# Block transposes on VectorE and DMAs between quadrants in place of TensorE transposes, in a two-layer graph kernel

## The chip, the cores and the metric

The kernel runs on one core of a Trainium2 chip. The metric is device time in microseconds (us); the time of a kernel is the median of its runs.

## The reference

x is 128 batches of 128 tokens by 512 features, adj is one 128 by 128 matrix, all float32. Both layers add a residual and normalize each row (mean and variance over the 512 features, eps 1e-5).

```
# layer 0
A = adj @ x[b];  C = adj @ x[b] + bias[:, None]
pre[o, m, n] = A[o, n] + (C - A)[o, m]
x1 = layernorm(x + max_n relu(pre))
# layer 1: 8 heads of 64, mask = adj
q, k, v = split(x1 @ w_qkv)
attn = softmax(where(adj == 0, -inf, q k^T / 8))
o = (attn @ v) @ w_proj + b_proj
out = layernorm(x1 + o + (layernorm(o) * gamma + beta))
```

In layer 0, both products use the same matrix, so C - A is the bias of the row and the maximum over n is the row maximum of adj @ x.

## The kernel before

All 128 batches pass through one software pipeline on the five engines. A tile holds one batch: 128 partitions (tokens) by 512 features. Batches go in groups of G = 4, whose 512 tokens form one moving operand for the projections to Q and K. The whole program is unrolled: the loop over steps s runs over the batches, and in one step TensorE works on different batches at different stages, as listed at the bottom of the kernel. A compiler layer derives the waits between engines and may reorder instructions of one engine by its own estimate of when they are ready.

In a step of the body TensorE runs, in this order: `scores` of batch s (pss, L198); one Q/K unit of the next group (pq, L158: four products of 128 by 128 by 512, each recorded as two instructions); `prob_transpose` of batch s - 1 (ptp, eight 128 by 128 transposes against the identity, L243); `layer0` of batch s + 9 (pa, L121); the second Q/K unit; `attend` of s - 1 (po, L255); `layer0_transpose` of batch s + 8 (ptx, four transposes, L147); `v_unit` (pv, L174); `project` of s - 1 (pp, L272). A matrix product contracts over the partitions, so the probabilities p and the layer-0 output x1 must be transposed before they can be operands: `prob_transpose` makes pT, read by `attend`, and `layer0_transpose` makes x1T, read by `qk_unit` and `v_unit`. Both write PSUM tiles, which ScalarE (L148, L245) and VectorE (L247) copy to SBUF.

Softmax: VectorE scales and masks the scores (L207) and takes the row maxima (L216), ScalarE runs eight exponentials (L222) with their sums, VectorE divides (L233, L235). Layer 0 after its product: a row maximum on VectorE (amax, L123), l0t = pa + bias on ScalarE (L125), minus pa on VectorE (L126), relu with amax on ScalarE (l0r, L128), plus x on GpSimd (y, L130). `stats` and `normalize` (L101 to L113) serve all layernorms, with the power on GpSimd; the tail of layer 1 uses GpSimd for gamma, beta and the sum (L285 to L287).

Transfers: x comes in by groups of four batches (1 MB each, L75) and the output leaves by batches (256 KB, L298), both on the queue of SP, in order; the weights are issued at the start on ScalarE's queue.

Of the kernel before, what the change touches and what calls it, by code (L numbers as in the profile page):

```python
# [16 lines left out]
def kernel(  # L17
# [12 lines left out]
    """Two residual+layernorm graph layers, software-pipelined over the batch.  # L30

    Batches go in groups of G, whose tokens share the moving operand of the
    Q/K projections. In step s the tensor engine works on
      batch s:             attention scores
      batch s - 1:         attention * V and the output projection
      group of s, plus 1:  a share of the Q/K/V projections
      batch s + 2G:        transposition of its layer-0 output
      batch s + 2G + 1:    the layer-0 product with adj
    so that each of these finds its operands ready.
    """  # L40
    nc = tc.nc
# [6 lines left out]
    NP = H // 2  # L48
    EPS = 1e-5
# [5 lines left out]
    ps_s = ctx.enter_context(tc.tile_pool(name="ps_s", bufs=2, space=bass.MemoryType.PSUM))  # L55
    ps_t = ctx.enter_context(tc.tile_pool(name="ps_t", bufs=2, space=bass.MemoryType.PSUM))
    ps_m = ctx.enter_context(tc.tile_pool(name="ps_m", bufs=3, space=bass.MemoryType.PSUM))
    ps_o = ctx.enter_context(tc.tile_pool(name="ps_o", bufs=1, space=bass.MemoryType.PSUM))

# [11 lines left out]
    xg = {}  # L71

    def load(g):
        t = sb.tile([P, G, D], F32, tag="xg", name=f"xg_{g}")
        nc.sync.dma_start(out=t, in_=x[ts(g, G)].rearrange("b p d -> p b d"))  # L75
        xg[g] = t

    load(0)
    load(1)

# [11 lines left out]
    # adj^T, and the additive mask: 0 on edges, and where adj is 0 a number so low  # L92
    # that exp(score - row maximum) is 0
    adjT = const.tile([P, P], F32, name="adjT")
    pt0 = ps_t.tile([P, KC, P], F32, tag="pt", name="pt0")
# [4 lines left out]

    def stats(src, name):  # L101
        """mean and (var + eps)^-0.5 of each row: [P, 2]"""
        st = small.tile([P, 6], F32, tag="st", name=f"st_{name}")
        nc.vector.bn_stats(st, src)  # L104
        mv = small.tile([P, 2], F32, tag="mv", name=f"mv_{name}", bufs=8)
        nc.vector.bn_aggr(mv, st)  # L106
        rs = small.tile([P, 1], F32, tag="rs", name=f"rs_{name}", bufs=8)
        nc.gpsimd.tensor_scalar(rs, mv[:, 1:2], EPS, None, ALU.add)  # L108
        nc.gpsimd.tensor_tensor(rs, rs, mhalf, ALU.pow)  # L109
        return mv, rs  # L110
# [5 lines left out]
    ys, y_st, x1s, x1T = {}, {}, {}, {}  # L116

    def layer0(f):
        xin = xg[f // G][:, f % G, :]
        pa = ps_m.tile([P, D], F32, tag="pm", name=f"pa_{f}")  # L120
        nc.tensor.matmul(pa, lhsT=adjT, rhs=xin, start=True, stop=True)  # L121
        amax = small.tile([P, 1], F32, tag="amax", name=f"amax_{f}")
        nc.vector.tensor_reduce(amax, pa, AX.X, ALU.max)  # L123
        t = sb.tile([P, D], F32, tag="l0t", name=f"l0t_{f}")
        nc.scalar.activation(t, pa, AF.Identity, bias=bias0)  # L125
        nc.vector.tensor_tensor(t, t, pa, ALU.subtract)  # L126
        r = sb.tile([P, D], F32, tag="l0r", name=f"l0r_{f}")
        nc.scalar.activation(r, t, AF.Relu, bias=amax)  # L128
        y = sb.tile([P, D], F32, tag="y", name=f"y_{f}")
        nc.gpsimd.tensor_tensor(y, xin, r, ALU.add)  # L130
        ys[f] = y
# [4 lines left out]
    def layer0_norm(f):  # L136
        x1 = sb.tile([P, D], F32, tag="x1", name=f"x1_{f}", bufs=2 * G + 6)
        normalize(x1, ys.pop(f), *y_st.pop(f))
        x1s[f] = x1

    def layer0_transpose(f):
        g, j = divmod(f, G)
        if j == 0:
            x1T[g] = sb.tile([P, KC, GT], F32, tag="x1T", name=f"x1T_{g}")
        pt = ps_t.tile([P, KC, P], F32, tag="pt", name=f"ptx_{f}")
        for c in range(KC):
            nc.tensor.transpose(pt[:, c, :], x1s[f][:, ts(c, P)], ident)  # L147
        nc.scalar.copy(x1T[g][:, :, ts(j, P)], pt)  # L148

# [1 line left out]
    qkT, vs = {}, {}  # L151

    def qk_unit(g, m):
        if m == 0:
            qkT[g] = sb.tile([P, 2 * KC, GT], F32, tag="qkT", name=f"qkT_{g}")
        pq = ps_m.tile([P, GT], F32, tag="pm", name=f"pq_{g}_{m}")
        for c in range(KC):
            nc.tensor.matmul(  # L158
                pq,
                lhsT=wqkv[:, c, ts(m, P)],  # L160
                rhs=x1T[g][:, c, :],
                start=(c == 0),
                stop=(c == KC - 1),
            )
        if m % 2 == 0:
            nc.scalar.copy(qkT[g][:, m, :], pq)
        else:
            nc.vector.tensor_copy(qkT[g][:, m, :], pq)

    def v_unit(f):  # L170
        g, j = divmod(f, G)
        pv = ps_m.tile([P, D], F32, tag="pm", name=f"pv_{f}")
        for c in range(KC):
            nc.tensor.matmul(  # L174
                pv,
                lhsT=x1T[g][:, c, ts(j, P)],
                rhs=wqkv[:, c, ds(2 * D, D)],
                start=(c == 0),
                stop=(c == KC - 1),
            )  # L180
        v = sb.tile([P, D], F32, tag="v", name=f"v_{f}", bufs=G + 3)
        nc.scalar.copy(v, pv)
        vs[f] = v

# [1 line left out]
    # Even and odd heads sit on the two halves of the array's rows and so write  # L186
    # to different PSUM banks: [:, parity, pair] is head 2 * pair + parity.
    sc, prob, psum_, pT, oT = {}, {}, {}, {}, {}

    def scores(b):  # L190
# [4 lines left out]
        for pr in range(NP):  # L195
            for par in range(2):
                rows = ds(par * HD, HD)
                nc.tensor.matmul(  # L198
                    pss[par][:, pr, :],
                    lhsT=qkT[g][rows, pr, ts(j, P)],  # L200
                    rhs=qkT[g][rows, KC + pr, ts(j, P)],
                    start=True,
                    stop=True,
                )
        s = sb.tile([P, 2, NP, P], F32, tag="s", name=f"s_{b}")
        for par in range(2):
# [9 lines left out]
        nc.vector.tensor_reduce(  # L216
            nmax, s.rearrange("p a h m -> p (a h) m"), AX.X, ALU.max, negate=True
        )
        sums = small.tile([P, H], F32, tag="sums", name=f"sums_{b}")
        p = sb.tile([P, 2, NP, P], F32, tag="prob", name=f"p_{b}")  # L220
        for i in range(H):
            nc.scalar.activation(  # L222
                p[:, i // NP, i % NP, :],
                s[:, i // NP, i % NP, :],
                AF.Exp,
                bias=nmax[:, i : i + 1],
                accum_out=sums[:, i : i + 1],
            )
        prob[b], psum_[b] = p, sums

    def softmax_div(b):
        rec = small.tile([P, H], F32, tag="rec", name=f"rec_{b}")
        nc.vector.reciprocal(rec, psum_.pop(b))  # L233
        p = prob[b].rearrange("p a h m -> p (a h) m")
        nc.vector.tensor_tensor(p, p, rec.unsqueeze(2).to_broadcast([P, H, P]), ALU.mult)  # L235

    def prob_transpose(b):
        p = prob.pop(b)
        t = sb.tile([P, 2, NP, P], F32, tag="pT", name=f"pT_{b}")
        for par in range(2):  # L240
            pt = ps_t.tile([P, NP, P], F32, tag="pt", name=f"ptp_{b}_{par}")
            for pr in range(NP):
                nc.tensor.transpose(pt[:, pr, :], p[:, par, pr, :], ident)  # L243
            if par == 0:
                nc.scalar.copy(t[:, par], pt)  # L245
            else:
                nc.vector.tensor_copy(t[:, par], pt)  # L247
        pT[b] = t

    def attend(b):  # L250
        v, t = vs.pop(b), pT.pop(b)
        po = ps_o.tile([P, NP, P], F32, tag="po", name=f"po_{b}")
        for pr in range(NP):
            for par in range(2):
                nc.tensor.matmul(  # L255
                    po[ds(par * HD, HD), pr, :],
                    lhsT=v[:, ds((2 * pr + par) * HD, HD)],
                    rhs=t[:, par, pr, :],
                    start=True,
                    stop=True,  # L260
                )
# [6 lines left out]
    def project(b):  # L268
        o = oT.pop(b)
        pp = ps_m.tile([P, D], F32, tag="pm", name=f"pp_{b}")  # L270
        for c in range(KC):
            nc.tensor.matmul(  # L272
                pp, lhsT=o[:, c, :], rhs=wproj[:, c, :], start=(c == 0), stop=(c == KC - 1)
            )
# [29 lines left out]
    for s in range(-(2 * G + 1), B + 4):  # L304
        g, j = divmod(s, G)
        nxt = g + 1
        has_next = 0 <= nxt < B // G
        on(scores, s)
        on(tail_outer, s - 3)
        on(layer0_norm, s + 2 * G)  # L310
        if has_next:
            qk_unit(nxt, 2 * j)
        on(prob_transpose, s - 1)
        on(layer0, s + 2 * G + 1)
# [4 lines left out]
        on(layer0_transpose, s + 2 * G)  # L319
        if has_next:  # L320
            v_unit(s + G)
        on(layer0_stats, s + 2 * G + 1)
        on(project, s - 1)
        on(softmax_div, s)
        on(tail_residual, s - 2)
        f = s + 2 * G + 1
        if f % G == G - 1 and 2 <= f // G + 2 < B // G:
            load(f // G + 2)
# [41 lines left out]
```

## Time and profile before

| | |
|---|---|
| median of 3 runs | 2444.42 us (2443.89 to 2444.57) |
| profiled execution, span | 2444.3 us |
| profiled execution around the span | nothing that shows: span and median agree within 0.2 us |
| TensorE busy | 2381.0 us, 97% of the span |
| VectorE / ScalarE / GpSimd busy | 59% / 37% / 39% |
| transfers | 73.95 MB, mean 30 GB/s; SP's queue takes 8.0% of the 16 DMA engines |
| granted TensorE clock, mean | 0.990 |

Times in the profile are of one execution. "Busy" sums the instructions of an engine; "idle before" is the time in which an engine waited ahead of a group of instructions, with what released it. The chain of work that ended last follows the execution back from its last instruction, at each step to what released it.

### The profile page before, as it was taken

Reading aid. Unit: us, or ns where it says so; the run is one execution under the profiler, and the core shown is the slowest. Engines: PE = TensorE matmul, PEld = TensorE weight load, DVE = VectorE, ACT = ScalarE, POOL = GpSimd, SP = SyncE. Lnnn points to the kernel's source line nnn. Section 1 sums busy time; section 2 is a strip of 40 time slices with the busy share of each in tenths; the row PEclk is TensorE's granted clock in tenths of the full one; section 3 lists DMA queues with packets and bytes.
Section 4 is the critical chain, followed back from the end, with each engine's and each line's share of the span. In section 5 each row is a group of like instructions: output and inputs, shape, how many; then the busy total and the mean of one; then the engine's idle time right before and its main releaser. Section 6 shows DMA issues by size and latency. Waiting matters only on the chain.

```text
span 2444.3 us, 28218 instructions
## 1 busy us (share of the span) xinstructions
PE 2381.0 (97%) x9985; PEld 1205.6 (49%) x9985; DVE 1449.8 (59%) x2562; ACT 899.4 (37%) x2945; POOL 951.7 (39%) x1287
## 2 busy tenths in 40 slices
PE   5999999999999999999999999999999999999995
PEld 2455455555555555545555555555554554555443
DVE  3465565666666656556566666666655656656556
ACT  2334334334333333333433433333333343343232
POOL 2134334334334334433433433433443343343335
PEclk8999999999999999999999999999999999999997
DMA  3000000000000001000000100100100000000000
GB/s 134 18 31 31 31 32 17 31 31 35 31 31 18 31 31 35 30 25 22 33 31 31 35 14 31 35 31 31 35 14 31 34 32 31 31 18 14 14 18 26
DMA packets 37292, 73.95 MB, mean 30 GB/s; under 512 B 2848, under 2 KB 2976, under 8 KB 37152
## 3 DMA queue, kind: packets, MB, share of 16 engines
q1 hardware_dynamic: 35616, 67.19, 8.0%
q10 hardware_dynamic: 1536, 4.98, 0.5%
q8 instruction: 78, 1.28, 0.2%
q14 instruction: 62, 0.51, 0.1%
HBM read 38.60 MB, written 33.55 MB: 30 GB/s over the span
## 4 chain that ended last, share of the span: by engine, by line
PE 94%; DVE 2%; POOL 2%; ACT 1%; DMA 1%; issue 0%; SPq 0%; POOLq 0%; ACTq 0%
PE pq L158 36%; PE pv L174 18%; PE pp L272 18%; PE po L255 6%; PE pss L198 5%; PE pa L121 5%; PE ptp L243 4%; PE ptx L147 3%; ACT p L222 1%; DMA xg<-in_x_dram 1%; POOL rs_o L109 0%; DVE nmax L216 0%; DVE o L276 0%; DVE st_o L104 0%; DVE st_z L104 0%
## 5 line engine op out<-in xcount | busy, mean ns | idle before, releaser
L158 PE MATMUL pq<-x1T,wqkv 128*128 128x512 f32 x2048 | 936.2, 600 | 0.7 <-ACT x1T L148 0.7
L222 ACT ACTIVATE p<-s,nmax 128x128 f32<-128x128 f32 x1024 | 396.3, 388 | 1053.3 <-DVE nmax L216 1053.3
L158 PEld LDWEIGHTS pq<-x1T,wqkv 128*128 128x128 f32 x2048 | 379.3, 190 | 445.3 <-issue 401.5
L272 PE MATMUL pp<-wproj,oT 128*128 128x512 f32 x1024 | 466.3, 598 | 1.5 <-ACT oT L263 1.5
L174 PE MATMUL pv<-wqkv,x1T 128*128 128x512 f32 x1024 | 461.0, 593 | 0.0
L130 POOL TENSOR_TENSOR y<-xg,l0r 128x512 f32<-128x512 f32 x128 | 162.5, 1270 | 499.3 <-ACT l0r L128 499.3
L272 PEld LDWEIGHTS pp<-wproj,oT 128*128 128x128 f32 x1024 | 196.5, 192 | 248.5 <-issue 245.1
L292 DVE TENSOR_TENSOR z<-z,x 128x512 f32<-128x512 f32 x128 | 88.6, 693 | 368.4 <-POOL z L287 368.4
L174 PEld LDWEIGHTS pv<-wqkv,x1T 128*128 128x128 f32 x1024 | 184.6, 190 | 184.3 <-issue 184.3
L285 POOL TENSOR_TENSOR z<-z,ga_bc 128x512 f32<-128x512 f32 x128 | 162.7, 1271 | 277.3 <-DVE z L113 277.3
L108 POOL TENSOR_SCALAR rs_o<-mv_o 128x1 f32<-128x1 f32 x128 | 27.5, 215 | 523.1 <-DVE mv_o L106 512.0
L104 DVE BATCH_NORM_STATS2 st_y<-y 128x6 f32<-128x512 f32 x128 | 88.9, 694 | 201.9 <-POOL y L130 201.9
L128 ACT ACTIVATE l0r<-l0t,amax 128x512 f32<-128x512 f32 x128 | 92.3, 722 | 299.4 <-DVE l0t L126 298.7
L222 ACT ACTIVATION_READ_ACCUMULATOR p<-s,nmax 128x1 f32 x1024 | 191.4, 187 | 0.0
L276 DVE TENSOR_TENSOR o<-pp,bp_bc 128x512 f32<-128x512 f32 x128 | 88.5, 692 | 153.4 <-PE pp L272 153.4
L198 PEld LDWEIGHTS pss<-qkT 64*128 64x128 f32 x2048 | 126.3, 188 | 96.6 <-issue 94.6
L255 PEld LDWEIGHTS po<-pT,v 128*64 128x64 f32 x2048 | 111.3, 138 | 122.3 <-ACT pT L245 109.1
L207 DVE SCALAR_TENSOR_TENSOR s<-pss,mask 128x512 f32<-128x512 f32 x256 | 168.0, 658 | 1.5 <-PE pss L198 1.5
L286 POOL TENSOR_TENSOR z<-z,be_bc 128x512 f32<-128x512 f32 x128 | 163.4, 1277 | 10.0
L287 POOL TENSOR_TENSOR z<-z,o 128x512 f32<-128x512 f32 x128 | 162.3, 1268 | 10.0
L255 PE MATMUL po<-pT,v 128*64 128x128 f32 x2048 | 143.5, 281 | 18.3 <-DVE pT L247 9.9
L235 DVE TENSOR_TENSOR p<-p,rec 128x1024 f32<-128x1024 f32 x128 | 157.4, 1230 | 4.2
(44 smaller groups left out, 2438.7 us busy)
## 6 DMA issues: line engine op xcount, KB each, us to landing
xg<-in_x_dram SPq DMA_DIRECT2D x32, 1024.0 KB, 5.3
out_dram<-res SPq DMA_DIRECT2D x128, 256.0 KB, 2.0
wqkv<-in_L_gnn_w_qkv_dram ACTq DMA_DIRECT2D x4, 768.0 KB, 8.7
wproj<-in_L_gnn_w_proj_dram ACTq DMA_DIRECT2D x1, 1024.0 KB, 14.1
bp_bc<-in_L_gnn_b_proj_dram ACTq DMA_DIRECT2D x1, 256.0 KB, 15.2
ga_bc<-in_L_gnn_ln_gamma_dram ACTq DMA_DIRECT2D x1, 256.0 KB, 15.0
be_bc<-in_L_gnn_ln_beta_dram ACTq DMA_DIRECT2D x1, 256.0 KB, 6.4
adj_sb<-in_adj_dram SPq DMA_DIRECT2D x1, 64.0 KB, 4.0
```

Source lines behind the costliest of these rows:

```text
L130: nc.gpsimd.tensor_tensor(y, xin, r, ALU.add)
L158: nc.tensor.matmul(pq, lhsT=wqkv[:, c, ts(m, P)], rhs=x1T[g][:, c, :], start=(c == 0), stop=(c == KC - 1),)
L174: nc.tensor.matmul(pv, lhsT=x1T[g][:, c, ts(j, P)], rhs=wqkv[:, c, ds(2 * D, D)], start=(c == 0), stop=(c == KC - 1),)
L198: nc.tensor.matmul(pss[par][:, pr, :], lhsT=qkT[g][rows, pr, ts(j, P)], rhs=qkT[g][rows, KC + pr, ts(j, P)], start=True, stop=True,)
L207: nc.vector.scalar_tensor_tensor(s[:, par], pss[par], SCALE, mask.unsqueeze(1).to_broadcast([P, NP, P]), ALU.mult, ALU.add,)
L222: nc.scalar.activation(p[:, i // NP, i % NP, :], s[:, i // NP, i % NP, :], AF.Exp, bias=nmax[:, i : i + 1], accum_out=sums[:, i : i + 1],)
L235: nc.vector.tensor_tensor(p, p, rec.unsqueeze(2).to_broadcast([P, H, P]), ALU.mult)
L255: nc.tensor.matmul(po[ds(par * HD, HD), pr, :], lhsT=v[:, ds((2 * pr + par) * HD, HD)], rhs=t[:, par, pr, :], start=True, stop=True,)
L272: nc.tensor.matmul(pp, lhsT=o[:, c, :], rhs=wproj[:, c, :], start=(c == 0), stop=(c == KC - 1))
L285: nc.gpsimd.tensor_tensor(z, z, ga_bc, ALU.mult)
L286: nc.gpsimd.tensor_tensor(z, z, be_bc, ALU.add)
L287: nc.gpsimd.tensor_tensor(z, z, o, ALU.add)
```

## The change

- `layer0_transpose` and `prob_transpose` no longer use TensorE. VectorE transposes each 32 by 32 block in place of its quadrant (32 partitions) into an intermediate tile, and `move_quadrants` then sends 16 DMAs, all on SP's queue, that carry block (i, q) from quadrant q to quadrant i. For the probabilities this is done for every batch (16 DMAs of 32 KB with 1 KB per partition); for x1 once per group of four batches (16 DMAs of 64 KB, whose destination consists of pieces of 128 bytes).
- The copies from PSUM (L148, L245, L247) go with it, and the two PSUM banks of the transposes go to the scores (3 instead of 2) and to the other products (4 instead of 3).
- In `layer0`, r is one number per row, max(amax + bias, 0), from one VectorE instruction on 128 by 1; y = x + r is one ScalarE instruction. The subtraction, the relu and the addition on GpSimd go.
- Layer 0 runs two steps further ahead (LA = 2G + 2 = 10), and x is loaded per batch into five buffers.
- The exponentials write in place of the scores. `prob_transpose` of batch s now stands at the end of step s instead of in step s + 1.
- `pin` keeps every TensorE product in program order.

```diff
-    ps_s = ctx.enter_context(tc.tile_pool(name="ps_s", bufs=2, space=bass.MemoryType.PSUM))
-    ps_t = ctx.enter_context(tc.tile_pool(name="ps_t", bufs=2, space=bass.MemoryType.PSUM))
-    ps_m = ctx.enter_context(tc.tile_pool(name="ps_m", bufs=3, space=bass.MemoryType.PSUM))
+    ps_s = ctx.enter_context(tc.tile_pool(name="ps_s", bufs=3, space=bass.MemoryType.PSUM))
+    ps_m = ctx.enter_context(tc.tile_pool(name="ps_m", bufs=4, space=bass.MemoryType.PSUM))
...
-    def load(g):
-        t = sb.tile([P, G, D], F32, tag="xg", name=f"xg_{g}")
-        nc.sync.dma_start(out=t, in_=x[ts(g, G)].rearrange("b p d -> p b d"))
-        xg[g] = t
+    def load(f):
+        t = sb.tile([P, D], F32, tag="x", name=f"x_{f}", bufs=5)
+        nc.sync.dma_start(out=t, in_=x[f])
+        xs[f] = t
...
+    pin = tc.keep_in_program_order
...
+    def move_quadrants(dst, src):
+        for i in range(Q):
+            for q in range(Q):
+                nc.sync.dma_start(out=dst[i][ds(q * QS, QS)], in_=src[q][ds(i * QS, QS)])
...
-        t = sb.tile([P, D], F32, tag="l0t", name=f"l0t_{f}")
-        nc.scalar.activation(t, pa, AF.Identity, bias=bias0)
-        nc.vector.tensor_tensor(t, t, pa, ALU.subtract)
-        r = sb.tile([P, D], F32, tag="l0r", name=f"l0r_{f}")
-        nc.scalar.activation(r, t, AF.Relu, bias=amax)
+        r = small.tile([P, 1], F32, tag="r", name=f"r_{f}")
+        nc.vector.tensor_scalar(r, amax, bias0, 0.0, ALU.add, ALU.max)
         y = sb.tile([P, D], F32, tag="y", name=f"y_{f}")
-        nc.gpsimd.tensor_tensor(y, xin, r, ALU.add)
+        nc.scalar.activation(y, xin, AF.Identity, bias=r)
...
         if j == 0:
-            x1T[g] = sb.tile([P, KC, GT], F32, tag="x1T", name=f"x1T_{g}")
-        pt = ps_t.tile([P, KC, P], F32, tag="pt", name=f"ptx_{f}")
-        for c in range(KC):
-            nc.tensor.transpose(pt[:, c, :], x1s[f][:, ts(c, P)], ident)
-        nc.scalar.copy(x1T[g][:, :, ts(j, P)], pt)
+            xts[g] = sb.tile([P, Q, KC, G, QS], F32, tag="xt", name=f"xt_{g}")
+        nc.vector.transpose(
+            xts[g][:, :, :, j].rearrange("p q c b -> p c q b"),
+            x1s[f].rearrange("p (c q a) -> p c q a", c=KC, q=Q),
+        )
+        if j == G - 1:
+            t, u = sb.tile([P, KC, G, Q, QS], F32, tag="x1T", name=f"x1T_{g}"), xts.pop(g)
+            move_quadrants([t[:, :, :, i] for i in range(Q)], [u[:, q] for q in range(Q)])
+            x1T[g] = t.rearrange("p c j i b -> p c (j i b)")
...
         p = prob.pop(b)
-        t = sb.tile([P, 2, NP, P], F32, tag="pT", name=f"pT_{b}")
-        for par in range(2):
-            pt = ps_t.tile([P, NP, P], F32, tag="pt", name=f"ptp_{b}_{par}")
-            for pr in range(NP):
-                nc.tensor.transpose(pt[:, pr, :], p[:, par, pr, :], ident)
-            if par == 0:
-                nc.scalar.copy(t[:, par], pt)
-            else:
-                nc.vector.tensor_copy(t[:, par], pt)
+        u = sb.tile([P, Q, H, QS], F32, tag="pu", name=f"pu_{b}")
+        nc.vector.transpose(
+            u.rearrange("p q h b -> p h q b"), p.rearrange("p h (q a) -> p h q a", q=Q)
+        )
+        t = sb.tile([P, Q, H, QS], F32, tag="pT", name=f"pT_{b}")
+        move_quadrants([t[:, i] for i in range(Q)], [u[:, q] for q in range(Q)])
         pT[b] = t
...
-                    rhs=t[:, par, pr, :],
+                    rhs=t[:, :, par * NP + pr, :],
...
-    for s in range(-(2 * G + 1), B + 4):
+    for s in range(-(LA + 1), B + 4):
...
+        if s > -(LA + 1):
+            on(load, s + LA + 3)
         on(scores, s)
         on(tail_outer, s - 3)
-        on(layer0_norm, s + 2 * G)
+        on(layer0_norm, s + LA)
+        on(layer0_transpose, s + LA)
         if has_next:
             qk_unit(nxt, 2 * j)
-        on(prob_transpose, s - 1)
-        on(layer0, s + 2 * G + 1)
+        on(layer0, s + LA + 1)
         if has_next:
             qk_unit(nxt, 2 * j + 1)
         on(tail_inner, s - 2)
         on(attend, s - 1)
-        on(layer0_transpose, s + 2 * G)
         if has_next:
             v_unit(s + G)
-        on(layer0_stats, s + 2 * G + 1)
+        on(layer0_stats, s + LA + 1)
         on(project, s - 1)
         on(softmax_div, s)
+        on(prob_transpose, s)
         on(tail_residual, s - 2)
```

## The prediction

> **What bounds the kernel now.** I read the page first: engine totals, and the shares of the chain of work that ended last.
>
> ```profile
> PE 2381.0 (97%) x9985; PEld 1205.6 (49%) x9985; DVE 1449.8 (59%) x2562; ACT 899.4 (37%) x2945; POOL 951.7 (39%) x1287
> PE 94%; DVE 2%; POOL 2%; ACT 1%; DMA 1%; issue 0%; SPq 0%; POOLq 0%; ACTq 0%
> ```
>
> TensorE carries 94% of the chain, so its own order of work sets the time. The table of stretches shows the same: the body, from the second scores to the end of layer 0, is 2179.47 us with TensorE busy 2176.01 of them. A body step is read from the chain in order of time (start, length, what):
>
> ```profile
> 1007.56 1.09 PE pss L198 x16
> 1008.65 3.63 PE pq L158 x8
> 1012.28 0.88 PE ptp L243 x8
> 1013.16 0.86 PE pa L121 x2
> 1014.02 3.43 PE pq L158 x8
> 1017.45 0.03 issue
> 1017.48 1.09 PE po L255 x16
> 1018.57 0.59 PE ptx L147 x4
> 1019.16 3.44 PE pv L174 x8
> 1022.60 3.43 PE pp L272 x8
> ```
>
> One step is 18.47 us with no gap but 0.03. Nothing in it waits for another engine. In the same stretch VectorE is busy 11.27 us of 18.47, ScalarE 6.99, GpSimd 7.41.
>
> The last step kind before the tail (stretch 2282 to 2373, no layer-0 work left) is different; the chain there is
>
> ```profile
> 2360.41 1.21 ACT p L222 x6
> 2361.88 1.73 ACT p L222 x9
> 2363.61 0.46 ACT qkT L166
> 2364.07 0.49 ACT pT L245
> 2364.56 0.04 issue
> 2364.61 1.09 PE po L255 x16
> 2365.70 3.63 PE pv L174 x8
> ```
>
> There the step takes 18.07 us (stretch: 90.40 for five), because the copy of pT stands on ScalarE behind eight exponentials. It also shows what pv costs straight after po: 3.63, not 3.44.
>
> For the transfers I read the queues' timelines and the landings:
>
> ```profile
> 0.72 0.39 SPq L67 DMA_DIRECT2D adj_sb<-in_adj_dram  x1
> 1.16 0.42 SPq L69 DMA_DIRECT2D bias<-in_L_gnn_b_dram  x1
> ...
> 6.61 0.54 ACTq L90 DMA_DIRECT2D ga_bc<-in_L_gnn_ln_gamma_dram  x1
> 15.83 0.34 ACTq L90 DMA_DIRECT2D be_bc<-in_L_gnn_ln_beta_dram  x1
> ...
> out_dram<-res SPq DMA_DIRECT2D x128, 256.0 KB, 2.0
> ```
>
> Back-to-back issues on SP start 0.44 us apart (0.72, 1.16; the next at 1.64, so 0.48). The twelfth transfer, be_bc, was ready to go at 7.15 and issued at 15.83, when the first load of x landed (the first pa, which needs it, starts at 15.94). The transfers' records name eight semaphores, used in turn, so at most eight are in flight and the issuing queue blocks on the ninth. A 256 KB store lands 2.0 us after issue.
>
> **TensorE, removed.** Per batch eight transposes of p (ptp, 0.88 us) and four of x1 (ptx, 0.59) go: 1.47. But po is then followed by pv directly, which the tail prices at 3.63 instead of 3.44. The new step is 1.09 + 3.63 + 0.86 + 3.43 + 0.03 + 1.09 + 3.63 + 3.43 = 17.19, a gain of 1.28. Pinning changes nothing I can price: the order shown is already that of the loop. po now reads p in four runs of 32; no row has such an operand. Bounds: 0 (same 128 columns) to 1.09 (every row at half speed); I take 0, as the count of columns is the same.
>
> **ScalarE and GpSimd.** ScalarE loses l0t (0.685), l0r (0.722), the x1T and one pT copy (0.587, 0.578), gains y at the price of l0r: 6.99 - 2.57 + 0.72 = 5.14. GpSimd loses y (1.27): 6.14. Neither is near 17.19.
>
> **VectorE.** It loses the subtraction (0.68) and one pT copy (0.68) and gains a 128x1 operation (about the reciprocal's 0.195) and two block transposes, 512 and 1024 elements a row. No row shows one. Nearest: one-input 512 at 0.54, two-input 512 at 0.69 and 1024 at 1.23. Lower end 0.54 + 1.08, upper end two passes, 1.38 + 2.46. I take 0.69 + 1.23. Total 11.27 - 1.36 + 0.20 + 1.92 = 12.0 of 17.19; upper end 13.9. It stays covered.
>
> **SP.** New: 16 transfers of 32 KB per batch for p, 16 of 64 KB per four batches for x1, one load and one store per batch: 22 a step, 34 in the step that closes a group. Issue: 0.33 (a lone store's row) to 1.15 (the longest issue in the page's load group); I take the back-to-back 0.46. That is 10.1 us a step, 15.6 in the group step, of 17.19. Eight in flight landing in 2.0 allow one per 0.25, so the limit of eight doesn't bind at that landing.
>
> **The wait that is new.** po(s) now needs 16 landings. Place them from the step that starts at 1210.64 (its pss): exponentials start at 1216.44, the division of p ends at 1222.95, 12.3 us into the step. Then 1.23 transpose, about 0.3 for hand-overs, 16 x 0.46 = 7.4 of issue, 2.0 landing: L = 23.2 after the scores. The transpose of x1 costs this chain nothing: after x is normalized at 1209.17 VectorE idles 1.03 us until pp ends. po(s) stands at 17.19 + 9.04 = 26.2. Margin 3.0 us. If L is longer, scores(s) to the next-but-one scores is L + 8.15 (po, pv, pp), so the step is (L + 8.15) / 2: it binds at L = 26.2 and eats the whole gain at 28.8.
>
> The group step: x1T's transfers start some 5 us into it and hold the rings ahead of p's. Each writes 512 rows of 128 bytes, 32 per ring. The packet records, by size, have medians of 9 ns (4 bytes), 25 to 27 (512) and 84 (2 KB). So a row of 128 bytes costs 9 ns at least and, as an upper bound, 84. I take the 14 of the straight line through 9 and 84: 16 x 32 x 14 = 7.2 us, no more than their issue. p's transfers follow unhindered.
>
> The Trainium skill speaks against both choices. "DMA: Bandwidth & Descriptors", section "Rules for kernel authors", says to coalesce, since under 64 KB one pays mostly overhead; were its 2.0 us fixed cost paid once per transfer in series, L would be 13.8 + 33 and the step 27 us. The trace has issues 0.44 us apart under landings of 2.0, so overhead overlaps. The same page's "Specifications" has read-modify-write below 512 bytes, while its "Why small descriptors are slow (HBM only)" exempts SBUF to SBUF; taken at twice the 512-byte packet the rows would cost about 52 ns, by the exemption nothing extra. No row here decides that.
>
> **Sum.** Profiled execution: span 2444.3, the median of the runs 2444.42, so nothing lies around it.
> - Before the first scores: 89.8 now. x arrives as three loads of 256 KB instead of one of 1 MB ahead of the first pa; x1's fourth normalization comes near 24 us instead of 39, plus 9.4 for the transfers gives the first pq at 33 against 40.7; the four steps then lose 2 us. Estimate -10, give or take 5.
> - First scores step 12.45 (12.89 less ptx).
> - Layer 0 now ends two steps earlier: 116 steps of 17.19 = 1994.0, then 7 without pa of 16.33 = 114.3. Before: 118 of 18.47 and 5 of 18.07.
> - Tail: 71.7 now. With little on TensorE, (L + po + pp)/2 with a shorter L of 20.6 gives 12.6 a step; the last po at about 57, pp at 61, then the 14.3 that follow the last pp now: 75.6, so +4 (-5 to +20).
> 79.8 + 12.45 + 1994.0 + 114.3 + 75.7 = 2276. With 0.1 a step either way the hidden case spans 2255 to 2310.
>
> **Rival 1, the issue on SP.** With p us per transfer L = 15.8 + 16p and the step is 12.0 + 8p; it binds at p = 0.65 and gives the old step at 0.81. SP's own total, 22p, does so at 0.84. For: 1.15 us issues exist, the fourth in a row at the start. Against: all store issues take 0.332 to 0.360. At p = 0.75 the step is 18.0 and the time about 2375; at 1.0 SP's total sets it, 22 us and 2870. I give it 2310 to 2500 mostly.
>
> **Rival 2, slower: rows of 128 bytes.** p's last eight transfers follow x1T's last landings: they land 5 + w + 5.7 into the group step, where w is x1T's time on the rings. po needs them at 26.2, so it binds at w = 15.5 (30 ns a row). The gain of 168 us is 5.25 per group, gone at 40 ns. At 49 ns, midway between 14 and 84, w = 25.1 and each of 32 groups loses 9.6: 2583; at 84 ns 27.5 each, 3150. For: no row here bounds 128-byte writes. Against: the 512-byte packets at 25 ns.
>
> **Rival 3, the gain is mostly eaten on TensorE itself.** Pinning and the shorter layer 0 are not on the chain, so only the removed transposes pay; if the strided operand of po costs 1.09 a step, 0.19 of the 1.28 is left: 124 x 1.09 = 135 more, 2411. Against it: its 128 columns stay the same; nothing for it but that no row shows it.
>
> **Chances.** Hidden 0.57; rival 1 0.16, three quarters of it still faster; rival 2 0.21, nearly all slower; strided po and others 0.06. 0.2% is 5 us, about what can be told from no change. Faster 0.68, within 0.03, slower 0.29. The range runs from 2250 to 2600 (rival 2 at about 50 ns): it leaves out the upper half of rival 2 and some hundredths below and in rival 1. The likeliest case's own range is 2255 to 2310, its time 2276.
>
> **What would show it.** Right: body steps of 17.2 on TensorE with no idle before po, ptp and ptx gone, transposes at 0.7 and 1.2, SP issues about 0.46 apart, landings near 2. Wrong: "PE po <- DMA pT" among the waits, every step for rival 1, once in four for rival 2 with x1T landings of many microseconds; po at 2 us for the strided operand; or VectorE above 15 us a step.

## The result and the profile after

The kernel after takes 2525.57 us (median of 4 runs, 2522.99 to 2529.62) against 2444.49 us before: a ratio of 1.0334, 95% interval 1.0320 to 1.0349. It is slower by 3.3%, where 2276 had been forecast. Its profiled execution has a span of 2524.1 us and a mean granted clock of 0.948 (before: 0.990).

The page's totals, and from its groups the line of `attend` (name, count, busy us, mean ns, idle before and its releaser):

```profile
PE 2278.5 (90%) x8449; PEld 1087.7 (43%) x8449; DVE 1532.6 (61%) x2690; ACT 700.1 (28%) x2561; POOL 787.9 (31%) x1159
...
L267 PE MATMUL po<-pT,v 128*64 128x128 f32 x2048 | 168.7, 315 | 197.6 <-DMA pT<-pu 188.9
```

The chain of work that ended last can be followed back over 18% of the span only; behind TensorE, SP's queue has the largest part of it, where it had 0% before:

```profile
PE 7%; SPq 5%; DVE 2%; POOL 2%; issue 1%; DMA 1%; ACT 0%; DVEq 0%; POOLq 0%; ACTq 0%
```

TensorE, 97% busy before, is now idle for 245.6 us, and 188.9 of these end when pT lands. TensorE's waits (us in total, times, longest) say how that is spread:

```profile
PE po L267 <- DMA pT<-pu: 188.9, 43, 8.6
PE pq L174 <- DMA x1T<-xt: 16.3, 1, 16.3
```

43 waits in 128 batches are not every step. From one pss to the next, steps take 17.19, 17.10, 24.04 and 17.10 us (medians by the step's place in its group): 75.4 a group, against 4 x 18.47 = 73.9 before. Three steps of four are as forecast, and one gives back more than all four gain. TensorE's timeline of that step (start, length, what; in brackets the idle time before it):

```profile
1179.14 1.16 PE L214 MATMUL pss<-qkT 64*128 64x128 f32 x16
1180.23 3.70 PE L174 MATMUL pq<-x1T,wqkv 128*128 128x512 f32 x8
1183.77 1.02 PE L135 MATMUL pa<-x,adjT 128*128 128x512 f32 x2
1184.63 3.60 PE L174 MATMUL pq<-x1T,wqkv 128*128 128x512 f32 x8
1193.82 1.98 PE L267 MATMUL po<-pT,v 128*64 128x128 f32 x16 [5.59 <-DMA pT<-pu]
1195.72 4.77 PE L190 MATMUL pv<-wqkv,x1T 128*128 128x512 f32 x8
1200.32 3.60 PE L284 MATMUL pp<-wproj,oT 128*128 128x512 f32 x8
1203.85 1.16 PE L214 MATMUL pss<-qkT 64*128 64x128 f32 x16
```

The step has 5.59 us of idle time, and then po takes 1.98 and pv 4.77 where they take 1.09 and 3.70 in the steps beside it: another 2.0. The windows of a step without and of this step with the stall (PE busy in the second number, PEclk third from the end) show the clock:

```profile
1161.94:1179.14 17.20, 17.17 (x67) 8.16 (x67) 11.94 (x21) 5.45 (x20) 6.14 (x9) 1.00 0.40 80
1179.14:1203.85 24.71, 19.12 (x68) 9.37 (x67) 11.94 (x21) 5.46 (x20) 6.13 (x9) 0.86 0.30 67
```

The granted clock is 1.00 and 0.86; inside the second window the trace has it at 0.50 for 6.83 us, from 1191.08 to 1197.91. What held pT back stands in the timeline of SP's queue of the same time:

```profile
1159.46 10.22 SPq L125 DMA_DIRECT2D pT<-pu  x16
1169.78 0.64 SPq L125 DMA_DIRECT2D x1T<-xt  x1
1170.52 0.56 SPq L310 DMA_DIRECT2D out_dram<-res  x1
1171.14 11.05 SPq L125 DMA_DIRECT2D x1T<-xt  x15
1182.30 10.07 SPq L125 DMA_DIRECT2D pT<-pu  x16
1192.47 0.53 SPq L310 DMA_DIRECT2D out_dram<-res  x1
1193.85 10.00 SPq L125 DMA_DIRECT2D pT<-pu  x16
...
1218.55 10.03 SPq L125 DMA_DIRECT2D pT<-pu  x16
```

Sixteen transfers of p hold the queue for 10 us. The second burst belongs to the scores of 1161.94; in a step without x1T p's first issue follows the scores by 14.7 us (1203.85 to 1218.55), so it was due at 1176.6. But x1T's sixteen came first. Their data was ready, as VectorE had written the last of xt by 1161.78, but they could not begin before the burst of the batch before had ended (1169.78, 7.8 us into the step of these scores); they and a store held the queue until 1182.2, and p began at 1182.30, 5.7 us late. These 5.7 us come back as the 5.59 of idle time before po, which stands in the next step, the one of 24.71 us. The third burst is on time again: by the scores of 1179.14 it is due at 1193.84, and SP is free at 1193.0.

The transfers are not slow on their way in the median. The tile views of SP's issues (ns minimum, median, maximum) and the page's landings (KB, median us from issue to landing):

```profile
L125 SPq DMA_DIRECT2D pT<-pu x2048: 507/588/1640, 97.8 to 2498.8; - x187
...
L125 SPq DMA_DIRECT2D x1T<-xt x512: 595/627/1992, 28.6 to 2315.8; - x171
```

```profile
pT<-pu SPq DMA_DIRECT2D x2048, 32.0 KB, 1.8
x1T<-xt SPq DMA_DIRECT2D x512, 64.0 KB, 2.3
```

From issue to issue inside a burst the median is 0.633 us for p and 0.672 for x1T.

### The profile page after: what moved, and what is told of

It is laid out like the page before. It is cut to its first block, busy times and chain, and to the rows that moved or that the text cites. A ratio compares the mean times of both kernels' runs of the same rounds, so it can differ in the third digit from the quotient of the medians.

```text
span 2524.1 us, 28394 instructions
## 1 busy us (share of the span) xinstructions
PE 2278.5 (90%) x8449; PEld 1087.7 (43%) x8449; DVE 1532.6 (61%) x2690; ACT 700.1 (28%) x2561; POOL 787.9 (31%) x1159
## 5 line engine op out<-in xcount | busy, mean ns | idle before, releaser
L236 ACT ACTIVATE s<-s,nmax 128x128 f32<-128x128 f32 x1024 | 396.1, 388 | 1093.2 <-DVE nmax L233 1093.2
L190 PE MATMUL pv<-wqkv,x1T 128*128 128x512 f32 x1024 | 509.5, 643 | 0.0
L267 PE MATMUL po<-pT,v 128*64 128x128 f32 x2048 | 168.7, 315 | 197.6 <-DMA pT<-pu 188.9
L190 PEld LDWEIGHTS pv<-wqkv,x1T 128*128 128x128 f32 x1024 | 199.9, 206 | 232.7 <-issue 229.5
L267 PEld LDWEIGHTS po<-pT,v 128*64 128x64 f32 x2048 | 134.5, 158 | 295.2 <-issue 270.1
L114 POOL TENSOR_SCALAR rs_y<-mv_y 128x1 f32<-128x1 f32 x128 | 28.3, 221 | 627.3 <-DVE mv_y L112 623.3
L198 ACT COPY v<-pv 128x512 f32<-128x512 f32 x128 | 74.9, 585 | 428.4 <-PE pv L190 428.4
L236 ACT ACTIVATION_READ_ACCUMULATOR s<-s,nmax 128x1 f32 x1024 | 191.4, 187 | 0.0
L249 DVE TENSOR_TENSOR s<-s,rec 128x1024 f32<-128x1024 f32 x128 | 156.8, 1225 | 4.4
L255 DVE STREAM_TRANSPOSE pu<-s 128x1024 f32<-128x1024 f32 x128 | 157.1, 1227 | 0.1
```

The source lines that it names most:

```text
L190: pin(nc.tensor.matmul(pv, lhsT=x1T[g][:, c, ts(j, P)], rhs=wqkv[:, c, ds(2 * D, D)], start=(c == 0), stop=(c == KC - 1),))
L236: nc.scalar.activation(p[:, i, :], p[:, i, :], AF.Exp, bias=nmax[:, i : i + 1], accum_out=sums[:, i : i + 1],)
L255: nc.vector.transpose(u.rearrange("p q h b -> p h q b"), p.rearrange("p h (q a) -> p h q a", q=Q))
L267: pin(nc.tensor.matmul(po[ds(par * HD, HD), pr, :], lhsT=v[:, ds((2 * pr + par) * HD, HD)], rhs=t[:, :, par * NP + pr, :], start=True, sto ...
```

## Theories and experiments

**The issue theory:** every transfer from SBUF to SBUF costs SP some 0.63 us of issue, and as the queue is in order, x1T's sixteen push p's sixteen behind the moment at which `attend` needs pT. **Its rival:** rows of 128 bytes make x1T's transfers slow, and p waits behind them on the DMA engines, however few issues there are. Times of before in these runs are 2444.0 to 2444.9.

**x1T in three portions.** The sixteen transfers of x1T are issued 6, 6 and 4 in three steps; number, sizes and rows stay.

```diff
-            move_quadrants([t[:, :, :, i] for i in range(Q)], [u[:, q] for q in range(Q)])
+            pend.extend(
+                (t[:, :, :, i][ds(q * QS, QS)], u[:, q][ds(i * QS, QS)])
+                for i in range(Q)
+                for q in range(Q)
+            )
...
+        some_quadrants(6 if s >= 0 else 16)
         on(tail_inner, s - 2)
```

(`some_quadrants(n)` issues the next n transfers of `pend`.)

> x1T's 16 transfers go out as 6, 6 and 4 in three successive steps, each lot in the middle of the step, ahead of p's; same transfers, same order of data. Theory A: per step SP then has 16 x 0.634 + 6 x 0.673 + 2 x 0.35 = 14.9 us of 17.1, p's first issue is no longer late, every step 17.1 to 17.4: 2300 to 2335. If SP's lots still push p by 1 us or more, the steps with a lot grow by up to half of it and the time is 2340 to 2400. A theory by which the total of SP's work sets the pace (22 issues on average, 14 us a step) expects the same.

Measured: 2325.45 us, ratio 0.9514 (0.9499 to 0.9528). By their place in the group, steps take 17.10 to 17.28 us in the median (single ones up to 18.3). SP's queue in a part of a group:

```profile
1169.08 10.21 SPq L125 DMA_DIRECT2D pT<-pu  x16
1179.39 0.53 SPq L321 DMA_DIRECT2D out_dram<-res  x1
1179.96 2.68 SPq L132 DMA_DIRECT2D x1T<-xt  x4
1182.74 1.04 SPq L79 DMA_DIRECT2D x<-in_x_dram  x2
1186.28 10.06 SPq L125 DMA_DIRECT2D pT<-pu  x16
```

The same transfers, with the same rows, lie in the gaps that p leaves, and 200 us are gone. So the place in the queue counts; whether x1T's issues or its rows fill that place, this run does not tell, and the next three do. TensorE executes the same 8449 instructions in 2217.9 us of busy time instead of 2278.5, at a mean granted clock of 0.981 instead of 0.948: 61 of the 200 us were the lower clock after the stalls (about 30 times the 2.0 us seen above), and 140 were idle time (245.6 less 105.6).

**x1T in four wide transfers.** Each carries 128 partitions and 256 KB, again in pieces of 128 bytes; the blocks stay in their quadrants, so x1T holds other numbers.

```diff
-            move_quadrants([t[:, :, :, i] for i in range(Q)], [u[:, q] for q in range(Q)])
+            for i in range(Q):
+                nc.sync.dma_start(out=t[:, :, :, i], in_=u[:, i])
```

> This kernel leaves out the move of x1's blocks between quadrants: 4 transfers of 128 partitions a group instead of 16 of 32, the same bytes and the same 8192 rows of 128 bytes, so x1T holds other numbers. Theory A (SP's issue: each transfer keeps SP 0.63 to 0.67 us, and x1T's 16 stand ahead of p's in one step of four): 4 issues take under 4 us, the step of 24.0 us goes back to 17.1 to 17.4, 29 times about 6.9 us less, 2300 to 2335. Theory B (the rows of 128 bytes or the bytes hold the rings, and the slow issue is back-pressure from them): the same rows need the same 11 us, the long step stays near 24, 2490 to 2525.

Measured: 2390.1 us, ratio 0.9776 (0.9756 to 0.9795), between both expectations; the group step is 19.14 us. The tile view of the issues:

```profile
L164 SPq DMA_DIRECT2D x1T<-xt x128: 606/1026/3491, 28.5 to 2178.2; - x128
```

At 0.65 us each, four issues would have held SP for 2.6 us. They take 1.03 us in the median and up to 3.5, and in the group at 1173.06 they and a store hold it for 7.2 us. So the number of issues isn't all, and the rows were tried by themselves.

**Rows of 2 KB instead of 128 bytes**, once in sixteen and once in four transfers (shown: sixteen). The blocks of x1T then stand in another order, so it holds other numbers.

```diff
+            flat = t.rearrange("p c j i b -> p (c j i b)")
-            move_quadrants([t[:, :, :, i] for i in range(Q)], [u[:, q] for q in range(Q)])
+            move_quadrants([flat[:, ts(i, D)] for i in range(Q)], [u[:, q] for q in range(Q)])
```

> x1T still goes in 16 transfers of 32 partitions on SP's queue, but each writes 2 KB in one piece per partition in place of 16 pieces of 128 bytes (the blocks of x1T then stand in another order, so the layer-1 results differ; instructions and waits are the same). Theory (16 issues of both ends in SBUF are the cost, whatever the rows): issue of x1T 0.60 to 0.65 us, group step 23 to 24.5 us, 2490 to 2530 as the kernel after. Rival (the rows of 128 bytes hold the queue): the stall before po goes, group step under 19 us, 2300 to 2350.

> As the run with x1T in 4 transfers of 128 partitions, but with 2 KB per partition in one piece in place of 16 pieces of 128 bytes (x1T holds other blocks, so the layer-1 results differ; instructions and waits are the same). Theory (what was left of the stall in that run, 2.82 us before po, was the rows holding the queue, issues of up to 3.5 us): issues 0.6 to 0.7 us each, group step 17.1 to 17.4, 2305 to 2335. Rival (any transfer of 256 KB holds the queue alike): issues of 1 us and more, group step 19 us, about 2390.

Measured: sixteen 2498.22 us (ratio 1.0222, 1.0192 to 1.0251), four 2316.7 us (0.9479, 0.9452 to 0.9507). The tile views, sixteen and then four:

```profile
L125 SPq DMA_DIRECT2D x1T<-xt x512: 507/588/2208, 29.0 to 2291.5; - x171
```

```profile
L165 SPq DMA_DIRECT2D x1T<-xt x128: 465/598/649, 28.1 to 2105.0; - x128
```

With sixteen transfers the group step stays at 23.60 us although the rows are sixteen times longer. With four and long rows it falls to 17.22. So the small rows cost some 27 us of the kernel's 2525.57 (0.04 us an issue), and matter more only where one transfer has 2048 of them. With the same rows of 2 KB, sixteen transfers instead of four cost 181 us.

The Trainium skill, "DMA: Bandwidth & Descriptors", section "Why small descriptors are slow (HBM only)", exempts transfers between SBUF and SBUF. For the 64 KB transfers that nearly holds (landing 2.3 us with 128-byte rows, 2.0 with 2 KB); for the 256 KB ones it does not (issue 1.026 us against 0.598, landing 4.7 against 2.5).

**p on two queues.** Every second transfer of p goes on ScalarE's queue, behind the copy of v.

```diff
+                if q % 2:
+                    pin(nc.scalar.dma_start(out=d, in_=s_))
+                else:
+                    nc.sync.dma_start(out=d, in_=s_)
```

> Eight of p's 16 transfers of each batch go to ScalarE's queue, behind the copy of v; x1T stays on SP. Theory A, with each queue issuing at its own pace: p needs 8 x 0.634 = 5.1 us on either, lands 21 us after the scores instead of 26, and x1T's 10.8 us fit in the step: all steps 17.1, 2290 to 2330. If the two queues share one generator at 0.63 us per transfer: 16 still need 10 us, the long step stays, 2480 to 2530. If ScalarE's eight issues (5 us of its idle 8) push the exponentials: 17.5 to 18.5 a step, 2350 to 2470.

Measured: 2306.39 us, ratio 0.9437 (0.9421 to 0.9453). The two queues work side by side:

```profile
1182.05 5.17 SPq L134 DMA_DIRECT2D pT<-pu  x8
...
1182.06 6.93 ACTq L132 DMA_DIRECT2D pT<-pu  x8
```

The median step takes 17.1 us (17.28 in the group step, single ones up to 18.7). Of TensorE's waits for pT 41.7 us are left, 33.5 of them after the last Q/K unit, where pT's latency sets the step. 219 us for moving eight issues: the Trainium skill ("DMA: Bandwidth & Descriptors", section "Issuing engines are not separate DMA queues") says that issuing from several engines saves only the sequencer's time, "usually small relative to the DMA itself". That it is this time agrees; that it is small does not hold here, where sixteen issues take 10 us and each transfer lands 1.8 us after its issue.

**The same with x1T's first two groups on two queues too.**

```diff
-            move_quadrants([t[:, :, :, i] for i in range(Q)], [u[:, q] for q in range(Q)])
+            (move_on_two_queues if g < 2 else move_quadrants)(
+                [t[:, :, :, i] for i in range(Q)], [u[:, q] for q in range(Q)]
+            )
```

> Every second transfer of p on ScalarE's queue, as in the run with p on two queues, and x1T's transfers of the first two groups as well. Theory (the issue time of SP's queue is the whole loss): the first scores start about 5 us earlier than in the run with p on two queues, because the first x1T's 16 issues of 0.67 us are split over two queues (10.8 us become 5.4); all else unchanged: 2301, between 2296 and 2306. Rival (landing of x1T is set by the rings, not by the issue): no earlier start, 2306.

Measured: 2308.03 us, ratio 0.9440 (0.9428 to 0.9453), no gain. The first scores start at 86.38 us against 88.57. In the first two groups the median landing of x1T rises from 2.3 to 3.4 us, so two queues of 64 KB transfers get in each other's way, which two of 32 KB did not (1.9 us on either, 1.8 on SP alone). In the profiled run the stretch after the first scores takes 5 us longer than with p alone on two queues; why stays open.

**x1 on TensorE again**, p still by VectorE and DMA. Layer 0 runs 8 steps ahead again instead of 10, and the transposes take one PSUM bank back from the scores.

```diff
+        pt = ps_t.tile([P, KC, P], F32, tag="pt", name=f"ptx_{f}")
+        for c in range(KC):
+            pin(nc.tensor.transpose(pt[:, c, :], x1s[f][:, ts(c, P)], ident))
+        nc.scalar.copy(x1T[g][:, :, ts(j, P)], pt)
```

> x1 is transposed on TensorE as before (four transposes, 0.59 us, and a ScalarE copy); p stays with VectorE and 16 transfers on SP. Theory (x1T's 16 issues ahead of p's in SP's queue cause the stall of the group step): no step of 24 us; every step 17.1 plus 0.59 less 0.19 = 17.5 us, so about 2360, between 2335 and 2375, and pT lands about 26 us after the scores in every step. Rival (the 16 transfers of p alone are already too late, whatever x1T does): stalls of 1 us and more in all steps, 2400 or more.

Measured: 2349.17 us, ratio 0.9610 (0.9597 to 0.9623); the median step is 17.49 us (single ones up to 18.47), the sum in the expectation. p's sixteen transfers alone are not too late: pT lands 26.0 us after the scores, and po follows pq without idle time.

```profile
1167.78 3.60 PE L171 MATMUL pq<-x1T,wqkv 128*128 128x512 f32 x8
1171.30 1.09 PE L264 MATMUL po<-pT,v 128*64 128x128 f32 x16
1172.33 0.66 PE L160 MATMUL ptx<-ident,x 128*128 128x128 f32 x4
1172.82 3.60 PE L187 MATMUL pv<-wqkv,x1T 128*128 128x512 f32 x8
```

**Layer 0 alone**, in the kernel before.

```diff
-        t = sb.tile([P, D], F32, tag="l0t", name=f"l0t_{f}")
-        nc.scalar.activation(t, pa, AF.Identity, bias=bias0)
...
+        r = small.tile([P, 1], F32, tag="r", name=f"r_{f}")
+        nc.vector.tensor_scalar(r, amax, bias0, 0.0, ALU.add, ALU.max)
...
+        nc.scalar.activation(y, xin, AF.Identity, bias=r)
```

> The kernel before with only the change of layer 0: one number per row and one ScalarE addition; transposes stay on TensorE. Theory (layer 0 is off the path that sets the end, TensorE's order does): 2444, within 5 us, with ScalarE about 0.7 us and VectorE and GpSimd 0.5 and 1.3 us a step less busy. Rival (shorter layer 0 shortens the path): 2425 or less.

Measured: 2441.05 us, ratio 0.9985 (0.9977 to 0.9994). ScalarE, VectorE and GpSimd lose 76, 76 and 162 us of busy time; steps stay at 18.48 us. What is gained lies at the start: in the profiled run (span 2437.7 us, 6.6 less) the first scores stand at 81.61 us instead of 89.77, and the rest takes 1.6 us longer.

**No pins.**

```diff
-    pin = tc.keep_in_program_order
+    def pin(ins):
+        return ins
```

> The kernel after without the pinned order of TensorE's products. Theory (the stall stands in SP's queue, and the order of TensorE is nearly the program's without the pins): 2500 to 2535, group step still near 24 us. Rival (the pins keep TensorE from doing other work while it waits for pT): 2400 or less, the group step at 19 us or less.

Measured: 2588.74 us, ratio 1.0589 (1.0573 to 1.0605), outside both expectations. Left to itself the order puts, once in a group, the next scores ahead of `attend`:

```profile
1229.23 1.60 PE L216 MATMUL pss<-qkT 64*128 64x128 f32 x20
1234.42 1.82 PE L216 MATMUL pss<-qkT 64*128 64x128 f32 x8 [3.59 <-DVE s L225]
1236.16 1.97 PE L269 MATMUL po<-pT,v 128*64 128x128 f32 x16
1240.01 5.78 PE L286 MATMUL pp<-wproj,oT 128*128 128x512 f32 x8 [1.88 <-ACT oT L277]
```

These scores wait 3.59 us for VectorE to empty a bank of the scores (31 such waits, 103.0 us), and pp then stands right behind po and waits for the copy oT (34 waits, 67.6 us). A group takes 78.5 us against 75.4. The pins are worth 63 us in this kernel. (The other PSUM banks and the two steps of lead for layer 0 were not tried by themselves.)

**What an issue costs.** A kernel of its own, without the two layers, puts twelve kinds of transfers twelve times each on SP's queue, and one of them on two queues.

> Not the layers: 12 transfers back to back of each of 12 kinds, a wait between kinds, then stores of one tile to every batch of the output. Asks what makes p's issue 0.588 us where a lone store's is 0.332. If the number of partitions (32): store and load of 32 partitions issue at 0.55 to 0.6 too, SBUF to SBUF with 128 partitions at 0.33 to 0.4. If both ends in SBUF: all SBUF to SBUF kinds at 0.5 to 0.6 whatever the partitions, stores and loads at 0.33 to 0.4. If back-pressure of the data: the 4 KB rows and 128 x 2 KB kinds at 0.7 to 0.9, 16 partitions at 0.35 to 0.45. Two queues at once: 0.6 each if side by side, 1.2 each if one generator serves both.

Measured from issue to issue, medians: SBUF to SBUF with 1 KB per partition 0.63 to 0.64 us for 16, 32, 64 and 128 partitions, in the own quadrant or another; 0.65 with 2 KB on 128 partitions. With one end in DRAM, 32 partitions of 1 KB: 0.46 either way. Where more bytes are on their way the issue varies: twelve 256 KB stores in a row slow down to 0.68, 256 KB loads go at 0.47, and SBUF to SBUF with 4 KB on each of 32 partitions, right behind those loads, takes 0.62 to 1.32. The tile view by direction, and two stretches of SP's queue (three kinds between SBUF and SBUF; one to DRAM):

```profile
L56 SPq DMA_DIRECT2D dst<-src x96: 507/589/616, 14.8 to 106.6; - x96
L56 SPq DMA_DIRECT2D dst<-in_x_dram x24: 328/426/592, 40.9 to 84.5; - x24
```

```profile
14.78 26.08 SPq L56 DMA_DIRECT2D dst<-src  x36
...
42.97 5.46 SPq L56 DMA_DIRECT2D out_dram<-src  x12
```

With both queues at once SP keeps 0.63 and ScalarE's takes 0.66 in the mean, so they share no such limit at 32 KB. At p's shape, 32 partitions of 1 KB, what decides is whether both ends are in SBUF. The startup rows from which the forecast took 0.46 have one end in DRAM.

**p through DRAM.** If an issue with one end in DRAM is cheaper and one transfer can take all 128 partitions, p can go out once and come back in four: 5 issues for 16.

```diff
+        d = dr.tile([P, Q, H * QS], F32, tag="pd", name=f"pd_{b}")
+        nc.sync.dma_start(out=d, in_=u.rearrange("p q h b -> p q (h b)"))
+        for q in range(Q):
+            nc.sync.dma_start(
+                out=t[ds(q * QS, QS)].rearrange("r i h b -> r i (h b)"),
+                in_=d[:, q].rearrange("(i r) f -> r i f", i=Q),
+            )
-        move_quadrants([t[:, i] for i in range(Q)], [u[:, q] for q in range(Q)])
```

> p goes to DRAM in one transfer of 128 partitions and comes back in four that read other quadrants' rows: 5 issues a batch on SP in place of 16, all with one end in DRAM, at the cost of a second trip. x1T stays as in the kernel after. Theory (issue time on SP is the loss): p holds SP for about 5 x 0.46 = 2.3 us plus the wait for its own store (2.5 to 4 us, from landings of 2.2 and 2.8 us for 256 KB), so x1T's 16 issues, 10.8 us, end before p of the same step is ready at 14.7 us; pT lands 21.5 to 24 us after the scores; all steps 17.1 to 17.4; 2290 to 2325. Rival (two trips through DRAM in series cost more than 16 issues): pT later than 26.2 us after the scores, steps of 18 us and more, 2400 or more.

Measured: 2695.12 us, ratio 1.1026 (1.1008 to 1.1045). The total is in the rival's range, but not its steps: three of four take 17.10 us, and the group step 30.62. SP's queue there:

```profile
1178.07 0.34 SPq L261 DMA_DIRECT2D pd<-pu  x1
1185.11 0.34 SPq L317 DMA_DIRECT2D out_dram<-res  x1
1195.17 0.32 SPq L261 DMA_DIRECT2D pd<-pu  x1
1195.59 4.32 SPq L263 DMA_DIRECT2D pT<-pd  x8
```

The store of one batch goes out at 1178.07. Its four loads stand behind the store of the next batch, which is ready only at 1195.17: the compiler layer had put SP's transfers in that order. Eight loads then go together, and po waits 11.73 us.

**The same with SP's transfers in the order of the program**, by a pin on each.

```diff
-        nc.sync.dma_start(out=d, in_=u.rearrange("p q h b -> p q (h b)"))
+        pin(nc.sync.dma_start(out=d, in_=u.rearrange("p q h b -> p q (h b)")))
```

(and so for the loads of pT and x, the store of the output and `move_quadrants`)

> As the run with p through DRAM, but all transfers on SP's queue stand in the order of the program text, so that the four loads of a batch's pT follow its own store at once and no longer stand behind the next batch's store. In the run before, three steps of four had pT landed about 22.5 us after the scores and took 17.10 us; the group step took 30.6, with SP idle 10 us ahead of the misplaced store. Theory (order in SP's queue, not the trip through DRAM, made that step late): x1T's issues end about 16 us into the group step, pT lands at 24 us or earlier, all steps 17.1 to 17.4; 2290 to 2325. Rival (the second trip beside x1T's 8192 pieces is what is slow): the group step stays above 20 us, 2400 or more.

Measured: 2290.61 us, ratio 0.9371 (0.9355 to 0.9386): the fastest version, 6.3% under the kernel before. Every step of the body takes 17.10 us.

```profile
1200.98 0.36 SPq L317 DMA_DIRECT2D out_dram<-res  x1
1201.43 12.03 SPq L126 DMA_DIRECT2D x1T<-xt  x16
1213.55 0.56 SPq L261 DMA_DIRECT2D pd<-pu  x1
1216.46 1.75 SPq L263 DMA_DIRECT2D pT<-pd  x4
```

x1T still holds SP for 12 us, but p now holds it for 4.7 from store to last load (1213.55 to 1218.21), and nothing is late.

## Why the prediction was wrong

**The step that failed** is in the paragraph on the group step: x1T's transfers would start 5 us into it, take no longer than their issue, and "p's transfers follow unhindered". They started 7.8 us into it, behind the burst of the batch before, held SP until 20.2, and p was due at 14.7. TensorE stalls for it one step later, at that batch's po. Thirty such steps exceed 17.1 us by 214 us together. Of the 248.1 by which the span missed 2276, the stretch from the first scores to those of batch 124 carries 215.

**The term that was mis-sized** is the issue, 0.46 us, measured 0.633 for p and 0.672 for x1T. It was taken from loads from DRAM, and the transfers that it priced go from SBUF to SBUF. The prediction put it between 0.33 and 1.15; it said of the block transposes, of po and of the small rows that no row showed them, but not of this one, and took the row that looked nearest by its place in a queue, not by its two ends.

**Rival 1 had the mechanism and lost it by averaging.** Its formula for L holds: 15.8 + 16 x 0.633 = 25.9, measured 26.0, just inside the 26.2 that po allows, which is why three steps of four run at 17.1. That it fits so well is partly luck: p's first issue comes 14.7 us after the scores and not 13.8, and the last landing 1.1 us after the burst and not 2.0. But it asked only for the mean step (bound at 0.65) and for SP's total. In the group step the order of the queue counts: p's burst of the batch before runs 14.7 + 16p - 17.1 into the step, x1T adds 16p, so this batch's p starts at 32p - 2.4, and pT lands 16p + 1.1 later. That is 48p - 1.3, and meets 26.2 at p = 0.57. At 0.633 it is 29.1, a stall of 2.9 us; most of the rest of the 5.59 is x1T itself, which with a store in between held SP for 12.4 us and not 10.1. By this order the forecast's 0.46 was 0.11 us an issue away from a stall in each group, not 0.19 as rival 1 had it. The chance of rival 1, 0.16, was too small for an unknown with bounds of 0.33 and 1.15.

**Rival 2 had the place and the wrong cause.** The stall is in the group step and behind x1T, as it said, but the rows of 128 bytes are 27 us of it, shown by the run with sixteen transfers of 2 KB rows. Their packets have a median of 13 ns in the kernel after, where the forecast took 14 and rival 2 needs 30. Waiting on SP's queue and waiting on the DMA engines look alike in the total; the timeline of SP separates them. The 2525.57 us lie inside the range given, 2250 to 2600, but it reached so high for rival 2's rows at about 50 ns: that is luck.

**What held.** The step on TensorE: forecast 17.19, measured 17.10. Strided po costs nothing (1.09 us), so rival 3 falls. VectorE's transposes take 1.227 and 0.711 us (forecast 1.23 and 0.69), its step 11.94 (12.0). The limit of eight transfers in flight does not bind: landings of 1.8 to 2.3 us against 5 us for eight issues.

**What was wrong beside it.** Pinning was priced at nothing; without it the kernel is 63 us slower still. The start: first scores at 87.58 us, not 79.8, since x1T's first transfer goes out at 28.64, the sixteen take 10.8, and the first pq starts at 41.4 (forecast 33).

The tail from the scores of batch 124 takes 100.7 us, not 75.7, and even in the fastest version 91.0: there each po waits for its pT (3.8 to 6.1 us), and pp, at a granted clock of 0.57 to 0.70, takes 5.2 to 6.8 us instead of 3.43, which the forecast, reckoning with 12.6 a step, did not have, although the tail of before has a granted clock of 0.79. In that version the body is 10.7 us shorter than forecast, the start and the tail 24.9 longer, so it ends 14 us over 2276, inside the range given for the hidden case (2255 to 2310): the sum priced a kernel whose transfers do not get in each other's way.

## What to carry to other kernels

Sum an in-order queue over the step with the most in it and by the order of its entries, not over the mean step: SP was held for 55 of 75 us in a group (an estimate from the medians from issue to issue), and that was enough for a stall of 5.6 us. When a block move needs many small transfers, price the issue from a row with the same two ends, and look first at the number of issues per engine and at what stands ahead of what; spreading, a second queue, and fewer transfers through DRAM in the right order each brought back 200 us or more here. A stall costs TensorE more than its length: 1.4 times here (200 us for 140 us of idle time).

## What the runs showed of the hardware

- From start to start, an issue from SBUF to SBUF with 1 KB per partition costs SP 0.63 to 0.64 us, for 16 to 128 partitions and whether or not the quadrant changes; with one end in DRAM, 32 partitions of 1 KB cost 0.46. A lone 256 KB store is issued in 0.33; twelve in a row go at up to 0.69.
- SP and ScalarE issue side by side for 32 KB transfers, at 0.63 and 0.64 us in the medians of the run with p on two queues.
- A transfer of 2048 rows of 128 bytes holds the issuing queue for 1.0 us in the median and up to 3.5; the same bytes in rows of 2 KB, 0.6.
- From 2.9 us after the start of an idle time of 5.59 us, the granted clock is 0.50 for 6.83 us. TensorE so ran at half speed for its first 4.1 us after the idle time: all of po (1.98 us for 1.09) and the beginning of pv (4.77 for 3.70).
